# Rows of x1 transposed by VectorE in the down stage's last pass instead of by TensorE in the attention

## The chip, the core and the metric

The kernel runs on one core of a Trainium2 chip. Its time is the device time of one execution in microseconds; the median of three runs counts. The engines are TensorE (PE, with its weight loads as PEld), VectorE (DVE), ScalarE (ACT), GpSimd (POOL) and SyncE (SP). SP, ACT and POOL also issue DMA transfers, each from a queue of its own that issues in order.

## The reference

One decoder layer over 16 sequences of 112 rows with 1024 columns, all in float32 but for the last product:

```
s  = silu(x @ w_gate.T)                     # 1792 rows x 2752
s  = s with the 1376 largest |s| of each row set to 0
x1 = layernorm(x + (s * (x @ w_up.T)) @ w_down.T)
q  = x1 @ Wq ; k, v = ctx @ Wk, ctx @ Wv    # 32 heads of 32, 8 key and value heads, 375 keys
x2 = layernorm(x1 + softmax(q k^T / sqrt(32)) v @ Wo)
out = layernorm(x2 + bf16(x2) @ bf16(dequantized 4-bit weights))
```

`x1` is needed twice: by rows, for the sum behind the attention, and with its columns on the partitions, as an operand of `x1 @ Wq`.

## The kernel before

The 1792 rows are 14 tiles of 128. The stages follow each other: gates with a search for each row's threshold, keys and values, up-projection, down-projection, attention with the last product. Every engine executes its instructions in the order in which the program was written (`as_written`); SP's and ACT's queues therefore issue their transfers in that order too.

**The down stage** (`Down`) takes the tiles in seven pairs j, and computes with sums of blocks in three passes. The last pass (`last_pass`, L652) does for each pair:

- `load_rest(j + 1)` (L646): SP loads two blocks `h` of the next pair from memory (640 KB and 48 KB each, L532 and L533), and DVE adds them (`combine`, L553 and L554). The buffers are those of the pair before, so a load has to wait for that pair's products. The next pair's first product uses the sum.
- the first product p, 11 matmuls of 128x512 (L546); DVE adds it to the second halves of both tiles' rows y0 and y1 (L683, L684); `norm(j, 0)` normalizes y0 on DVE (L72 to L80, with one step on POOL, L75), and POOL stores it to `x1_d` (L672).
- `load_rows(j + 1)` (L659): SP loads the next pair's rows of `x` (L662).
- the second product q; DVE subtracts it from the first half of y1 (L689); `norm(j, 1)`.
- `add_rows(j + 1)` (L665): POOL adds three partial results, `c11`, `v` and `u`, to the next rows (L668, four adds).
- the steps of `beside[j]`. Eight of them unpack the 4-bit weights on DVE (`compute` in `unpack_steps`, L716): a cast, and twice four shifts, one subtraction (L727) and one multiplication (L728). They stand at pairs 1, 1, 2, 3, 4, 4, 5, 6. Their loads are 17 small transfers on ACT's queue each (`load`, L706), at pairs 0, 0, 1, 1, 2, 3, 4, 4. ACT also loads `wq` in four parts.

**x1 transposed** (`Queries`, L735). A group is two sequences, 224 rows. `fetch` (L743) loads one sequence's 112 rows from `x1_d` by ACT's queue into `xr`, of which there is one buffer. `rows` (L748) lets PE transpose them in eight blocks of 112x128 (L757) and ACT copy them from PSUM to `x1T` (L758). `chunk` (L760) multiplies one of eight parts of `wq` with the group's `x1T` (8 matmuls of 224 columns, L765). Group 0 is fetched and turned inside the last pass (`beside[4]` to `beside[6]`), so the transposes stand in PE's order between the products of pair 5 and pair 6 and behind those of pair 6. Three chunks follow, and then the attention.

**The attention** runs 128 units n. Each has four score matmuls (L832), maxima on DVE (L838), exponentials on ACT (L840), a division on POOL (L849) and a 32x32 transposition on DVE (L860); every second unit, 16 transfers (11 on SP, 5 on POOL, L874) put the squares in place for the values' matmuls (L887). The chunks of the next groups, the projection with `wo` (L924), the norms and the last product (L975) are put between the units. At its start SP loads keys (L811), values (L815), `wo` in 16 parts (L999), and then the next keys. The remaining fetches and transposes of x1 stand between the units as well (L1071 to L1078).

Of the kernel before, what the change touches and what calls it, by code (L numbers as in the profile page):

```python
# [10 lines left out]
F32 = mybir.dt.float32  # L11
# [11 lines left out]
P = 128  # L23
B, S, D = 16, 112, 1024
NT = B * S
TT = NT // P
KC = D // P
# [3 lines left out]
Q = 32  # L31
NKQ = -(-SK // Q)
SKP = NKQ * Q
NKP = -(-SK // P)
NH, NKV, HD = 32, 8, 32
REP = NH // NKV
KVD = NKV * HD
GB = 2
GT = GB * S
# [431 lines left out]
class Down:  # L471
# [12 lines left out]

    def __init__(self, nc, tc, negh, wd, hT_d, x, x1_d, ps):
        self.nc, self.tc, self.negh, self.wd, self.hT_d = nc, tc, negh, wd, hT_d
        self.x, self.x1_d, self.ps = x, x1_d, ps
        self.pairs = TT // 2  # L490
        self.parts = {"11": [], "21": []}
        self.asked = [(b, k) for b in ("11", "21") for k in range(HK)]
        self.n_blocks = 0
        self.live = {}
# [154 lines left out]
        self.combine(self.nc.vector, a21, a21, a22, ALU.add)  # L649
        self.live[j] = a21, a22  # L650

    def last_pass(self, beside):  # L652

        nc = self.nc
        with ExitStack() as ctx:
            ld = ctx.enter_context(self.tc.tile_pool(name="d_ld", bufs=4, side="right"))
            small = ctx.enter_context(self.tc.tile_pool(name="d_small", bufs=2, side="right"))

            def load_rows(j):  # L659
                ys = [ld.tile([P, D], F32, tag="y", name=f"y_{j}_{i}") for i in range(2)]  # L660
                for i, y in enumerate(ys):
                    nc.sync.dma_start(y, self.x[ts(2 * j + i, P), :])  # L662
                return ys

            def add_rows(j, ys):  # L665
                for i, h, c in ((0, 0, self.c11), (0, 1, self.v), (1, 1, self.u), (1, 0, self.u)):
                    y = ys[i][:, ts(h, 512)]
                    nc.gpsimd.tensor_tensor(y, y, c[j], ALU.add)  # L668

            def norm(j, i, y):  # L670
                layer_norm(nc, small, y, y, self.negh)
                nc.gpsimd.dma_start(self.x1_d[ts(2 * j + i, P), :], y)  # L672

            rows = {0: load_rows(0)}
            add_rows(0, rows[0])
            for j in range(self.pairs):
# [6 lines left out]
                nc.vector.tensor_add(y0[:, 512:], y0[:, 512:], p)  # L683
                nc.vector.tensor_add(y1[:, 512:], y1[:, 512:], p)  # L684
                norm(j, 0, y0)
                if j + 1 < self.pairs:
                    rows[j + 1] = load_rows(j + 1)
                self.product(q, a22, lambda k: self.chunk("21", k))
                nc.vector.tensor_tensor(y1[:, :512], y1[:, :512], q, ALU.subtract)  # L689
# [45 lines left out]
class Queries:  # L735


    def __init__(self, nc, tc, ctx, ident, x1_d, wq_sb, bank):
        self.nc, self.ident, self.x1_d, self.wq_sb, self.bank = nc, ident, x1_d, wq_sb, bank
        self.pool = ctx.enter_context(tc.tile_pool(name="q_work", bufs=1, side="right"))  # L740
        self.x1T, self.qT, self.xr = {}, {}, {}

    def fetch(self, g, bb):  # L743

        self.xr[g, bb] = self.pool.tile([S, D], F32, tag="xr", name=f"xr_{g}_{bb}")
        self.nc.scalar.dma_start(self.xr[g, bb], self.x1_d[ds((g * GB + bb) * S, S), :])

    def rows(self, g, bb):  # L748
        nc = self.nc
        if bb == 0:  # L750
            self.x1T[g] = self.pool.tile([P, KC, GT], F32, tag="x1T", name=f"x1T_{g}")
            self.qT[g] = self.pool.tile([P, KC, GT], F32, tag="qT", name=f"qT_{g}", bufs=2)
        xr = self.xr.pop((g, bb))
        for k0 in range(0, KC, 4):
            pt = self.bank()[:, : 4 * S].rearrange("p (k s) -> p k s", k=4)
            for k in range(4):
                nc.tensor.transpose(pt[:, k, :], xr[:, ts(k0 + k, P)], self.ident[:S, :S])  # L757
            nc.scalar.copy(self.x1T[g][:, k0 : k0 + 4, ts(bb, S)], pt)  # L758

    def chunk(self, g, mc):  # L760

        nc = self.nc
        pq = self.bank()
        for kc in range(KC):
            nc.tensor.matmul(  # L765
                pq[:, :GT], self.wq_sb[:, kc, ts(mc, P)], self.x1T[g][:, kc, :],
                start=(kc == 0), stop=(kc == KC - 1),
            )
        nc.scalar.activation(self.qT[g][:, mc, :], pq[:, :GT], AF.Copy, scale=SCALE)


def attention_and_ffn(nc, tc, ident, ident_b, negh, x1_d, k_d, v_d, queries, wf_sb, wo, out):
# [16 lines left out]
    with ExitStack() as ctx:  # L789
# [201 lines left out]
        per_group = n_units // (B // GB)  # L991
# [9 lines left out]


        asked, behind, light = deque((0, mc) for mc in range(EARLY, KC)), deque(), {}
        turned, fetched = GB, GB
        sums, tails = {}, {}
        done = soon = 0

# [45 lines left out]
        for n in range(n_units):  # L1053
            b, c, r = units[n]
            if n % 4 == 1 and n // 4 + 1 < 2 * B:
                load_keys(*divmod(n // 4 + 1, 2))
            sums[n] = scores(n)
            if n:
                normalize(n - 1, sums.pop(n - 1))
            if n > 1:  # L1060
                square(n - 2)

            due = asked and n >= asked[0][0] * per_group + asked[0][1] - 2
            if due or (not piece(n) and asked):
                queries.chunk(*asked.popleft())
            if n == 0:
                queries.chunk(*asked.popleft())
            if n > LAG and (n - LAG) % 2:
                attend(n - LAG)

            if not asked and turned < B and n >= (turned // GB - 1) * per_group:  # L1071
                queries.rows(turned // GB, turned % GB)
                turned += 1
                if turned % GB == 0:
                    asked.extend((turned // GB - 1, mc) for mc in range(KC))
            if fetched == turned < B:
                queries.fetch(fetched // GB, fetched % GB)
                fetched += 1  # L1078
            lights(n)
            if done + len(tails) < soon and Tail.live < 3:  # L1080
                tails[done + len(tails)] = Tail(done + len(tails))
# [39 lines left out]
def kernel(  # L1121
# [29 lines left out]
    k_d = dram.tile([B, P, 2, SK], F32, tag="k", name="k_d")  # L1151
    v_d = dram.tile([B, SKP, KVD], F32, tag="v", name="v_d")
    x1_d = dram.tile([NT, D], F32, tag="x1", name="x1_d")

    hT_d = [dram.tile([P, 2 * HK, P], F32, tag=f"h{t}", name=f"hT_d{t}") for t in range(TT)]
    with as_written(nc, tc):
        with ExitStack() as psum:
            ps_g = psum.enter_context(tc.tile_pool(name="ps_g", bufs=6, space=PSUM))
            ps_t = psum.enter_context(tc.tile_pool(name="ps_t", bufs=2, space=PSUM))
            with ExitStack() as left:  # L1160
                down = Down(nc, tc, negh, wd, hT_d, x, x1_d, ps_g)
# [8 lines left out]
                queries = Queries(nc, tc, ctx, ident, x1_d, wq_sb, lambda: down.bank("pq"))  # L1170
                with tc.tile_pool(name="q", bufs=2, side="right") as q_pool:

                    def load_wq(i):
                        nc.scalar.dma_start(wq_sb[:, :, ts(i, D // 4)], wq[:, :, ts(i, D // 4)])

                    loads, computes = unpack_steps(nc, q_pool, wf_sb, qw, qs, qz)
                    beside = [[] for _ in range(TT // 2)]
                    for i, j in enumerate((1, 1, 2, 3, 4, 4, 5, 6)):
                        beside[j].append(computes[i])
                    for i, j in enumerate((0, 0, 1, 1, 2, 3, 4, 4)):  # L1180
                        beside[j].append(loads[i])
                    for i in range(4):
                        beside[i // 2].append(lambda i=i: load_wq(i))
                    beside[4].append(lambda: queries.fetch(0, 0))
                    beside[5] += [lambda: queries.rows(0, 0), lambda: queries.fetch(0, 1)]
                    beside[6].append(lambda: queries.rows(0, 1))
                    down.last_pass(beside)
            for mc in range(EARLY):
                queries.chunk(0, mc)
        attention_and_ffn(nc, tc, ident, ident_b, negh, x1_d, k_d, v_d, queries, wf_sb, wo, out)  # L1190
# [48 lines left out]
```

## Time and profile before

| | |
|---|---|
| median of three runs | 2656.92 us (2655.61 to 2657.28) |
| the profiled execution | 2661.48 us, span 2659.7 us, mean granted clock 0.983 |
| PE, DVE, ACT, POOL busy | 97%, 65%, 52%, 40% of the span |
| last pass of the down stage | from about 1735 us to 1891 us of the span |
| first scores of the attention | 1901.95 us |
| last scores | 2595.7 us |
| transposes of x1 on PE | 128, in 16 blocks of 8, from 1868.2 to 2463.2 us |
| copies of them on ACT | 32, 0.54 us each |

Times in the profile are microseconds from the start of the span, and L numbers are lines of the kernel. A group's row gives the operation, what it writes and reads, how often, and its mean duration. The views of waits say which instruction stood still until which other one had ended; for SP, what its queue waited for before it could issue. Windows give each engine's busy time, the granted clock and the share of the DMA engines in a stretch.

### The profile page before, as it was taken

What the parts mean: (1) busy time and instruction counts of PE and PEld (TensorE: products, weight loads), DVE (VectorE), ACT (ScalarE), POOL (GpSimd) and SP (SyncE); (2) the same over time, 40 slices, a digit from 0 to 9 for tenths busy, and PEclk for the clock granted to TensorE, in tenths of its full rate; (3) what the DMA queues carried; (4) which work ended last, traced back from release to release, by engine and by line L of the source; (5) the groups of instructions that cost most, each with busy time, mean ns of one, the idle gap of its engine ahead of it and who ended that gap; (6) DMA issues with size and microseconds to landing.
All of it is one profiled execution on the core that took longest, in us unless ns stands there. A gap on an engine that the chain in (4) does not pass through costs nothing.

```text
span 2659.7 us, 33179 instructions
## 1 busy us (share of the span) xinstructions
PE 2584.9 (97%) x10266; PEld 1482.7 (56%) x10266; DVE 1730.8 (65%) x3579; ACT 1377.6 (52%) x2413; POOL 1053.8 (40%) x1097
## 2 busy tenths in 40 slices
PE   9999999999999999999999999998899999999997
PEld 4444444577776555555554444443556666667663
DVE  0478778866876788788730343158467777777773
ACT  0487787777767777787610000000255555565553
POOL 0002022213322444344450000023277888788783
PEclk9999999999999999999999999999889999999998
DMA  6221223154443543443346222166567777777763
GB/s 253 94 74 56 77 91 126 51 195 168 181 169 136 162 140 121 143 132 117 95 145 228 86 96 94 59 204 202 133 169 196 196 191 193 192 205 194 188 175 103
DMA packets 216960, 387.70 MB, mean 146 GB/s; under 512 B 32080, under 2 KB 151120, under 8 KB 212688
## 3 DMA queue, kind: packets, MB, share of 16 engines
q1 hardware_dynamic: 165456, 257.19, 32.3%
q0 software_dynamic: 35840, 100.59, 11.6%
q10 hardware_dynamic: 15488, 27.80, 3.5%
q8 instruction: 83, 1.36, 0.2%
q14 instruction: 93, 0.76, 0.1%
HBM read 208.36 MB, written 76.43 MB: 107 GB/s over the span
## 4 chain that ended last, share of the span: by engine, by line
PE 90%; DVE 3%; DMA 3%; ACT 2%; issue 1%; POOL 1%; ACTq 0%; SPq 0%; POOLq 0%; DVEq 0%
PE pg L146 20%; PE pu L234 19%; PE m L546 14%; PE bank L924 7%; PE pk L184 6%; PE pk L176 6%; PE bank L765 6%; PE sc L832 4%; PE po L887 3%; PE bank L975 2%; PE pt L255 1%; ACT probs L840 1%; DVE b L727 1%; DMA xr<-x_d 1%; DVE nmax L838 1%
## 5 line engine op out<-in xcount | busy, mean ns | idle before, releaser
L284 ACT ACTIVATE ja<-a,cand 128x1824 int8<-128x1824 f32 x434 | 788.6, 1817 | 178.4 <-DVE cand L296 174.4
L287 DVE TENSOR_SCALAR_CACHE_REDUCE jv<-a,cand 128x928 uint8<-128x928 f32 x434 | 510.0, 1175 | 56.9 <-ACT a L271 48.8
L234 PE MATMUL pu<-wu_sb,uxT 128*128 128x512 f32 (+1 forms) x1344 | 530.6, 548 | 0.0
L146 PE MATMUL pg<-wg_sb,gxT 128*128 128x456 f32 (+1 forms) x1344 | 519.9, 550 | 5.9 <-DMA wg_sb<-in_wg_dram 5.9
L840 ACT ACTIVATE probs<-sc,nmax 128x375 f32<-128x375 f32 x512 | 287.4, 573 | 237.6 <-DVE nmax L838 218.2
L146 PEld LDWEIGHTS pg<-wg_sb,gxT 128*128 128x128 f32 x1344 | 256.2, 191 | 268.8 <-issue 265.3
L849 POOL TENSOR_TENSOR probs<-probs,sums 128x1500 f32<-128x1500 f32 x128 | 344.2, 2689 | 142.4 <-DVE sums L848 123.2
L234 PEld LDWEIGHTS pu<-wu_sb,uxT 128*128 128x128 f32 x1344 | 249.0, 190 | 230.0 <-issue 188.4
L838 DVE TENSOR_REDUCE nmax<-sc 128x2 f32<-128x750 f32 x256 | 228.6, 932 | 150.3 <-PE sc L832 150.2
L546 PE MATMUL m<-wd,h 128*128 128x512 f32 (+1 forms) x616 | 268.0, 597 | 0.0
L860 DVE STREAM_TRANSPOSE squares<-probs 128x1536 f32<-128x1536 f32 x128 | 224.0, 1750 | 9.7 <-DMA weights<-squares 5.5
L155 POOL DMA_DIRECT2D s_d<-s x84 | 46.0, 548 | 427.4 <-DVE s L154 351.5
L765 PE MATMUL bank<-x1T,wq_sb 128*128 128x224 f32 x976 | 202.6, 361 | 0.0
L546 PEld LDWEIGHTS m<-wd,h 128*128 128x128 f32 (+1 forms) x616 | 117.5, 191 | 149.2 <-issue 145.1
L765 PEld LDWEIGHTS bank<-x1T,wq_sb 128*128 128x128 f32 x976 | 181.3, 191 | 33.2 <-issue 30.2
L924 PE MATMUL bank<-wo_sb,aT 128*128 128x256 f32 x832 | 195.0, 388 | 0.0
L758 ACT COPY x1T<-pq 128x448 f32<-128x448 f32 x4 | 2.0, 535 | 371.6 <-PE pq L757 371.6
L874 POOL DMA_DIRECT2D weights<-squares x320 | 178.6, 564 | 9.0 <-issue 6.6
L924 PEld LDWEIGHTS bank<-wo_sb,aT 128*128 128x128 f32 x832 | 155.4, 192 | 46.5 <-issue 24.9
L184 PE MATMUL pk<-wv_sb,ctx 128*128 128x256 f32 (+1 forms) x768 | 168.4, 379 | 0.0
L176 PE MATMUL pk<-ctx,wk_sb 128*128 128x375 f32 x512 | 164.4, 478 | 0.0
L184 PEld LDWEIGHTS pk<-wv_sb,ctx 128*128 128x128 f32 (+1 forms) x768 | 144.0, 188 | 24.8
(118 smaller groups left out, 2881.8 us busy)
## 6 DMA issues: line engine op xcount, KB each, us to landing
weights<-squares SPq DMA_DIRECT2D x704, 96.0 KB, 3.3
h<-hT_d SPq DMA_DIRECT2D x56, 640.0 KB, 4.5
weights<-squares POOLq DMA_DIRECT2D x320, 96.0 KB, 3.4
ctx<-in_ctxT_dram SPq DMA_DIRECT2D x16, 1500.0 KB, 6.7
a<-s_d SPq DMA_DIRECT2D x14, 1376.0 KB, 7.9
us<-s_d SPq DMA_DIRECT2D x56, 256.0 KB, 2.7
hT_d<-hT POOLq DMA_DIRECT2D x56, 256.0 KB, 3.1
s_d<-s POOLq DMA_DIRECT2D x56, 228.0 KB, 2.2
```

Source lines behind the costliest of these rows:

```text
L146: nc.tensor.matmul(pg[:, :w], xts[t][:, kc, :], wg_sb[:, kc, ds(off, w)], start=(kc == 0), stop=(kc == KC - 1),)
L176: nc.tensor.matmul(pk[:, :SK], wk_sb[:, kc, ts(u, P)], c[:, kc, :], start=(kc == 0), stop=(kc == KC - 1),)
L184: nc.tensor.matmul(pk[:n, :KVD], c[:, kc, ds(at, n)], wv_sb[:, kc, :], start=(kc == 0), stop=(kc == KC - 1),)
L234: nc.tensor.matmul(pu[:, :w], xts[t][:, kc, :], wu_sb[0][:, kc, ds(off, w)], start=(kc == 0), stop=(kc == KC - 1),)
L284: nc.scalar.activation(ja, a[:, NV:], AF.Sign, bias=cand, scale=-1.0, accum_out=st["sgn"])
L287: nc.vector.tensor_scalar(jv, a[:, :NV], cand, -(TOPK - 1 - NA / 2), ALU.is_lt, ALU.add, accum_out=st["nlt"])
L546: self.nc.tensor.matmul(bank, a[:r, k, :], b(k)[:r], start=(k == 0), stop=(k == HK - 1),)
L765: nc.tensor.matmul(pq[:, :GT], self.wq_sb[:, kc, ts(mc, P)], self.x1T[g][:, kc, :], start=(kc == 0), stop=(kc == KC - 1),)
L838: nc.vector.tensor_reduce(nmax[h], sc[h][:, :, :SK], AX.X, ALU.max, negate=True)
L840: nc.scalar.activation(pr[:, i, :SK], sc[i // 2][:, i % 2, :SK], AF.Exp, bias=nmax[i // 2][:, i % 2 : i % 2 + 1], accum_out=sums[:, i : i ...
L849: nc.gpsimd.tensor_tensor(pr, pr, sums.unsqueeze(2).to_broadcast([P, 4, SK]), ALU.mult)
L924: nc.tensor.matmul(pp[:, :256], aT[:, h, r, :], wo_sb[:, h * REP + r, ts(i, 256)], start=(h == 0 and r == 0), stop=(h == 1 and r == REP - 1),)
```

## The change

`x1` is stored a second time, transposed in 32x32 squares, in a new array `x1T_d` of 128 partitions, 56 blocks of 32 rows, 8 parts of columns and 32 rows. In `norm`, after each tile has been normalized, DVE transposes its two halves (128x512 each) square by square, into buffers that are no longer needed (`c11`, `v` and `u` of the pair) and, for the fourth half, into a new one, `x1sq`. Four transfers on SP's queue store each half, one for each 32 partitions: 64 KB each, in runs of 512 bytes.

`Queries.load` takes the place of `fetch` and `rows`: one load of a group (128 partitions of 7 KB, 896 KB) by ACT's queue. The matmul of a chunk reads its 224 columns as seven runs of 32. PE's transposes and ACT's copies are gone. Group 0's load stands at pair 4, later ones in the attention as soon as the chunks of the group before are done; this moves some of the chunks and pieces of projection by a unit.

The steps that unpack weights move from `beside[j]` to `amid[j]`: after y0's norm, ahead of the subtraction of the second product, in the same pairs as before.

```diff
             def norm(j, i, y):
                 layer_norm(nc, small, y, y, self.negh)
-                nc.gpsimd.dma_start(self.x1_d[ts(2 * j + i, P), :], y)
+                t = 2 * j + i
+                nc.gpsimd.dma_start(self.x1_d[ts(t, P), :], y)
+                to = self.x1T_d.rearrange("(m p) b k f -> p m b k f", p=Q)
+                n = KC // 2
+                for h in range(2):
+                    sq = ((self.c11[j], self.v[j]), (self.u[j], None))[i][h]
+                    if sq is None:
+                        sq = ld.tile([P, 512], F32, tag="sq", name=f"x1sq_{t}", bufs=1)
+                    sq = sq.rearrange("p (m k f) -> p m k f", m=SQ, f=Q)
+                    nc.vector.transpose(
+                        sq, y[:, ts(h, 512)].rearrange("p (k m f) -> p m k f", m=SQ, f=Q)
+                    )
+                    for b in range(SQ):
+                        nc.sync.dma_start(to[:, :, t * SQ + b, ts(h, n)], sq[ts(b, Q)])
...
                 norm(j, 0, y0)
+                for step in amid[j]:
+                    step()
                 if j + 1 < self.pairs:
                     rows[j + 1] = load_rows(j + 1)
...
-    def fetch(self, g, bb):
-
-        self.xr[g, bb] = self.pool.tile([S, D], F32, tag="xr", name=f"xr_{g}_{bb}")
-        self.nc.scalar.dma_start(self.xr[g, bb], self.x1_d[ds((g * GB + bb) * S, S), :])
-
-    def rows(self, g, bb):
...
-        for k0 in range(0, KC, 4):
-            pt = self.bank()[:, : 4 * S].rearrange("p (k s) -> p k s", k=4)
-            for k in range(4):
-                nc.tensor.transpose(pt[:, k, :], xr[:, ts(k0 + k, P)], self.ident[:S, :S])
-            nc.scalar.copy(self.x1T[g][:, k0 : k0 + 4, ts(bb, S)], pt)
+    def load(self, g):
+
+        n = GT // Q
+        self.x1T[g] = self.pool.tile([P, n, KC, Q], F32, tag="x1T", name=f"x1T_{g}")
+        self.nc.scalar.dma_start(self.x1T[g], self.x1T_d[:, ts(g, n)])
...
             nc.tensor.matmul(
-                pq[:, :GT], self.wq_sb[:, kc, ts(mc, P)], self.x1T[g][:, kc, :],
+                pq[:, :GT].rearrange("p (b f) -> p b f", f=Q), self.wq_sb[:, kc, ts(mc, P)],
+                self.x1T[g][:, :, kc, :],
...
-            if not asked and turned < B and n >= (turned // GB - 1) * per_group:
-                queries.rows(turned // GB, turned % GB)
-                turned += 1
-                if turned % GB == 0:
-                    asked.extend((turned // GB - 1, mc) for mc in range(KC))
-            if fetched == turned < B:
-                queries.fetch(fetched // GB, fetched % GB)
-                fetched += 1
+            if not asked and group < B // GB:
+                if group not in queries.x1T:
+                    queries.load(group)
+                elif n >= (group - 1) * per_group:
+                    asked.extend((group, mc) for mc in range(KC))
+                    group += 1
...
-                    beside = [[] for _ in range(TT // 2)]
+                    amid, beside = ([[] for _ in range(TT // 2)] for _ in range(2))
                     for i, j in enumerate((1, 1, 2, 3, 4, 4, 5, 6)):
-                        beside[j].append(computes[i])
+                        amid[j].append(computes[i])
...
-                    beside[4].append(lambda: queries.fetch(0, 0))
-                    beside[5] += [lambda: queries.rows(0, 0), lambda: queries.fetch(0, 1)]
-                    beside[6].append(lambda: queries.rows(0, 1))
-                    down.last_pass(beside)
+                    beside[4].append(lambda: queries.load(0))
+                    down.last_pass(amid, beside)
```

More of the change, by code (lines that the diff above doesn't have):

```diff
@@ L34 @@
 NKP = -(-SK // P)
+SQ = P // Q
 NH, NKV, HD = 32, 8, 32
@@ L471, with __init__ @@
 class Down:
-    def __init__(self, nc, tc, negh, wd, hT_d, x, x1_d, ps):
+    def __init__(self, nc, tc, negh, wd, hT_d, x, x1_d, x1T_d, ps):
         self.nc, self.tc, self.negh, self.wd, self.hT_d = nc, tc, negh, wd, hT_d
-        self.x, self.x1_d, self.ps = x, x1_d, ps
+        self.x, self.x1_d, self.x1T_d, self.ps = x, x1_d, x1T_d, ps
         self.pairs = TT // 2
@@ L650, in load_rest, with last_pass @@
         self.live[j] = a21, a22
-    def last_pass(self, beside):
+    def last_pass(self, amid, beside):
         nc = self.nc
@@ L735, with __init__ @@
 class Queries:
-    def __init__(self, nc, tc, ctx, ident, x1_d, wq_sb, bank):
-        self.nc, self.ident, self.x1_d, self.wq_sb, self.bank = nc, ident, x1_d, wq_sb, bank
+    def __init__(self, nc, tc, ctx, x1T_d, wq_sb, bank):
+        self.nc, self.x1T_d, self.wq_sb, self.bank = nc, x1T_d, wq_sb, bank
         self.pool = ctx.enter_context(tc.tile_pool(name="q_work", bufs=1, side="right"))
-        self.x1T, self.qT, self.xr = {}, {}, {}
-    def fetch(self, g, bb):
-        self.xr[g, bb] = self.pool.tile([S, D], F32, tag="xr", name=f"xr_{g}_{bb}")
-        self.nc.scalar.dma_start(self.xr[g, bb], self.x1_d[ds((g * GB + bb) * S, S), :])
-    def rows(self, g, bb):
[L749 to L753, printed above, removed]
-        for k0 in range(0, KC, 4):
-            pt = self.bank()[:, : 4 * S].rearrange("p (k s) -> p k s", k=4)
-            for k in range(4):
-                nc.tensor.transpose(pt[:, k, :], xr[:, ts(k0 + k, P)], self.ident[:S, :S])
-            nc.scalar.copy(self.x1T[g][:, k0 : k0 + 4, ts(bb, S)], pt)
+        self.x1T, self.qT = {}, {}
+    def load(self, g):
+        n = GT // Q
+        self.x1T[g] = self.pool.tile([P, n, KC, Q], F32, tag="x1T", name=f"x1T_{g}")
+        self.nc.scalar.dma_start(self.x1T[g], self.x1T_d[:, ts(g, n)])
     def chunk(self, g, mc):
         nc = self.nc
+        if g not in self.qT:
+            self.qT[g] = self.pool.tile([P, KC, GT], F32, tag="qT", name=f"qT_{g}", bufs=2)
         pq = self.bank()
@@ L1003, in attention_and_ffn @@
         asked, behind, light = deque((0, mc) for mc in range(EARLY, KC)), deque(), {}
-        turned, fetched = GB, GB
+        group = 1
         sums, tails = {}, {}
@@ L1153 @@
     x1_d = dram.tile([NT, D], F32, tag="x1", name="x1_d")
+    x1T_d = dram.tile([P, NT // Q, KC, Q], F32, tag="x1T", name="x1T_d")
     hT_d = [dram.tile([P, 2 * HK, P], F32, tag=f"h{t}", name=f"hT_d{t}") for t in range(TT)]
@@ L1160 @@
             with ExitStack() as left:
-                down = Down(nc, tc, negh, wd, hT_d, x, x1_d, ps_g)
+                down = Down(nc, tc, negh, wd, hT_d, x, x1_d, x1T_d, ps_g)
                 gates_keys_up(
@@ L1169 @@
                 wf_sb = a_w.tile([P, 8, D], BF16, tag="wf", name="wf_sb")
-                queries = Queries(nc, tc, ctx, ident, x1_d, wq_sb, lambda: down.bank("pq"))
+                queries = Queries(nc, tc, ctx, x1T_d, wq_sb, lambda: down.bank("pq"))
                 with tc.tile_pool(name="q", bufs=2, side="right") as q_pool:
```

## The prediction

> **What bounds the kernel now.** I read the page's engine shares and its chain first, to see whether TensorE (PE) sets the time.
>
> ```profile
> PE 2584.9 (97%) x10266; PEld 1482.7 (56%) x10266; DVE 1730.8 (65%) x3579; ACT 1377.6 (52%) x2413; POOL 1053.8 (40%) x1097
> PE 90%; DVE 3%; DMA 3%; ACT 2%; issue 1%; POOL 1%; ACTq 0%; SPq 0%; POOLq 0%; DVEq 0%
> ```
>
> PE bounds nearly everything. The change touches the last pass of the down stage and the attention, so I next asked for busy time by stretch:
>
> ```profile
> 1812.00:1831.00 19.00, 19.00 (x45) 8.21 (x45) 17.23 (x29) 0.00 (x0) 7.23 (x8) 1.00 0.78 260
> 1850.00:1868.00 18.00, 0.00 (x0) 0.00 (x0) 16.26 (x28) 0.00 (x0) 7.21 (x8) 0.61 0.31 101
> 1902.00:1930.00 28.00, 21.19 (x124) 18.00 (x128) 10.77 (x14) 13.08 (x40) 10.79 (x8) 0.92 0.74 171
> 2350.00:2550.00 200.00, 199.69 (x1433) 142.16 (x1432) 152.31 (x197) 117.91 (x371) 165.74 (x152) 1.00 0.77 198
> ```
>
> (Columns: length; PE, PEld, DVE, ACT, POOL busy; clock; DMA share; GB/s.) In the last pass PE is full, and VectorE (DVE) is busy 17.2 of 19 us, nearly a second bound. PE then stands still for 18 us, and again for 7 us where the attention starts; later it is full. The waits of 1763 to 1903 us name the first hole:
>
> ```profile
> PE pq L757 <- DMA xr<-x_d: 18.7, 1, 18.7
> PEld m L546 <- DVE h L553: 2.4, 3, 0.9
> ```
>
> The rows to be transposed arrive late. The products hardly wait for the combined blocks `h`. DVE's timeline over one pair:
>
> ```profile
> 1809.76 1.48 DVE L553 TENSOR_TENSOR h<-h,h 128x1280 f32<-128x1280 f32 x1
> 1811.36 0.68 DVE L683 TENSOR_TENSOR y<-y,m 128x512 f32<-128x512 f32 x1
> 1815.72 0.68 DVE L689 TENSOR_TENSOR y<-y,m 128x512 f32<-128x512 f32 x1
> 1819.57 0.22 DVE L719 CAST zf<-zi 128x128 f32<-128x128 int32 x1
> 1820.37 5.69 DVE L727 TENSOR_TENSOR b<-b,zf 128x512 f32<-128x512 int32 x1
> 1828.82 1.49 DVE L553 TENSOR_TENSOR h<-h,h 128x1280 f32<-128x1280 f32 x1
> ```
>
> The lap is 19.06 us: combine 1.60, adds and first norm 4.36, subtraction and second norm 3.85, unpacking 9.25. PE needs 18.9 (22 products of 128x512 at 0.859, from 1754.4 to 1773.3). The laps just fit. Last I asked what SP's queue waits for, because the change puts stores there:
>
> ```profile
> SPq L811 <- PE m L546: 28.2, 1, 28.2
> SPq L532 <- DMA zi<-in_qz_dram: 21.4, 3, 15.6
> SPq L533 <- DMA sc<-in_qs_dram: 13.6, 3, 5.6
> SPq L811 <- DMA xr<-x_d: 9.9, 1, 9.9
> ```
>
> Loads of `h` wait for small loads of another queue that they don't use: in the built order each transfer from SP or ACT waits for the one eight before it. `h` waits so, with q, y and further zi and sc, 51.3 us over seven pairs, about 7 each. Today that is hidden.
>
> **PE transposes and ScalarE copies go.** Sixteen blocks of eight transposes leave PE: 14 in the attention at 0.93 us (row at 1921.66) are 13.0 us of a full PE, with 10.7 us of waits for `xr` (5.6 and 5.1). Two leave the last pass, with the 18.7 us hole and about 2.5 us in which PE then ran at half clock (clock 0.50 from 1868 to 1874; the products took 21.4 us instead of 18.9). 32 copies of 0.54 us leave ACT, which isn't the bound: nothing.
>
> **VectorE gains 56 instructions, four per pair.** The attention's L860 takes 1750 ns for 1536 columns, so 512 columns take 0.58 us; 0.69 is the upper end (a 512-column add). I take 0.58: 2.33 us per pair.
>
> On the Trainium skill: the page "VectorE: DVE Perf Modes", section "Rules for kernel authors", advises TensorE for a 128x128 transpose where PSUM will do. Its section "The three transpose paths" gives 311 ns on VectorE against 390 on TensorE for a bf16 block. By those figures eight blocks in each of 14 tiles would gain an estimated 9 us. This trace has 116 ns a block on PE (0.93/8) and 146 on DVE (1.17/8), so by the rows the move loses 3.4 us of engine time. The measurement decides; neither figure is used below.
>
> **Unpacking moves ahead of the second product's subtraction.** Each of eight blocks has 14 DVE instructions and no DMA. Beside POOL's adds its L727 takes 5.69 us, alone 0.69; the undisturbed block from 1786.42 to 1790.67 took 4.25. POOL's adds now fall after the second norm, beside transposes and a wait, so I take 4.25 (up to 9.25 if they still meet). The move delays the second norm by 4.25, or 8.5 in pairs 1 and 4, which unpack twice.
>
> **112 stores join SP's queue, and they carry the cost.** Per pair SP now issues: stores of y0 (8), loads of the next y (2), stores of y1 (8), and only then the `h` loads (4) for the pair after next. Before, the `h` loads waited for PE alone and came a lap early. Now they stand behind stores that wait for the second norm, the combine waits for `h`, and all DVE work of the next lap stands behind the combine. A store of 64 KB isn't in the trace. Issue lies between 0.37 (the `h` load) and 0.65 (weights on SP, eleven in 7.11 us); I take 0.65, also 32 partitions per transfer. Landing is 2.2 to 3.3 us.
>
> The new lap, combine to combine: 1.60 + 4.36 + two transposes 1.17 + unpacking 4.25 + 3.85 + one transpose 0.58 = 15.8 us to the first y1 store; then 8 x 0.65 = 5.2, four issues 1.5, landing 4.4 (median here): 26.9. To this come the eight-back waits. At least 0, at most some 10, since 16 transfers of about 3 us share the rotation with today's 7; I take 5, below today's 7, since some of those waits overlap the stores: **32 us a lap**. With two unpackings, 4.25 more for DVE and 2.2 for the second set of 17 loads: **38.5**.
>
> The second norm of pair 0 ends at 1758.4. One transpose, 11.1 of return and 5 of waits put pair 2's combine at 1775 (before: 1761.6). Laps of 38.5, 32, 32 and 38.5 bring pair 6's to 1916, and its first product to 1917.7. Before it began at 1869.7: **+48.0**. The two products then take 21.4 as before, after idle time as before.
>
> **The keys stand behind the last stores.** Before, kT was issued at 1891.18, as the last product ended. Now subtraction and norm 3.85, a transpose 0.58 and eight stores 5.2 come first: 9.6 later. The three query chunks (9.35 us) cover the first keys but for 1.2 us. The second keys follow the 16 wo loads (24.2 us), and PE already waits 6.8 for them, so all **+9.6** shows.
>
> **One x1T load of 896 KB per group replaces two of 448.** Landing lies between 4.8 (`xr`) and 7.9 (1376 KB rows). Each holds one of the eight places for longer, and keys and weights wait behind. The attention gains at most 23.7 and loses at worst 10. I keep the 13.0 and give 8 back: **-5.0**. Query products now read seven runs of 32 columns; L887, which also reads such runs, takes 391 ns against 388 contiguous, so nothing (1.7 us at most). Group 0's load is issued two products before its use and is covered.
>
> **Sum:** 48.0 + 9.6 - 5.0 = +52.6 us. The profiled run took 2661.48 (span 2659.7, 1.8 around it), 4.6 above the median 2656.92. A profile of the new kernel should show some 2714; the median becomes 2709.
>
> **Rivals.**
> - *The return trip is hidden: faster.* Should `h` go out early enough, PE's 18.9 remain, the hole goes, and the last product ends at 1868.4 instead of 1891.1: -22.7 + 9.6 - 23.7 = -36.8, 2620 us. It decides where the four laps fall below 22.1 us on average ((141 - 52.6)/4). For it: today `h` goes out early. Against: 15.8 + 5.2 + 1.5 + 4.4 is already above.
> - *A bare return, without eight-back waits.* Laps of 26.9 and 31.2 from 1770 put the last combine at 1886.2, its product at 1887.9: +18.2 + 9.6 - 5.0 = +22.8, 2680 us. For it: landings can be 2.2 us. Against: the waits of SP shown above.
> - *Waits of 10 a lap.* Laps of 37 and 43.5 from 1780 put the last product at 1942.7: +73.0 + 9.6, with the attention between -5 and +10: 2735 to 2750 us. For it: stores wait for zi and sc loads, and these for stores.
>
> **How the numbers follow.** The round trip with waits of 3 to 8 us: 0.55. Bare: 0.17. Long: 0.16. Hidden: 0.09. Cancelled to within 0.2%: 0.02. Another slower way: 0.01. About 0.2%, 5 us, is what a measurement of this kernel can tell from no change. Slower 0.89, same 0.02, faster 0.09. The range 2664 to 2744 leaves out the hidden case and half of the long one.
>
> **What would show it.** Right: PE idle 10 to 20 us before each of the products of pairs 2 to 6, released by L554's `h`; DVE waiting for `h<-hT_d`; `h` issued after the stores of x1sq; L745 near 0.69 us; kT issued some 10 us after the last product. Wrong: `h` issued during the first product of the lap before, laps near 19 us, or an attention that is longer than before by more than 10 us. The prediction fails if stores issue much faster than 0.65, or the eight-back waits fall beside DVE's work instead of after it.

## The result, and the profile after

The changed kernel takes 2698.1 us (median of four runs, 2697.1 to 2707.7), the kernel before in the same session 2657.1 (2655.6 to 2659.7). The ratio is 1.0161, with a 95% interval of 1.0137 to 1.0186: 41 us slower. The profiled execution of the changed kernel took 2707.71 us (span 2705.9), 9.6 above its median; the sums below are made from it and, as in the prediction, against the profiled execution of before (span 2659.7): +46.2 us.

First the shares of the engines and the chain, from the page of the changed kernel:

```profile
PE 2575.8 (95%) x10124; PEld 1470.4 (54%) x10138; DVE 1724.6 (64%) x3607; ACT 1359.0 (50%) x2381; POOL 1052.6 (39%) x1097
...
PE 84%; DMA 5%; DVE 4%; issue 2%; ACT 2%; SPq 1%; POOL 1%; ACTq 0%; POOLq 0%; DVEq 0%
```

PE's busy time fell by only 9 us, and its share of the chain from 90% to 84%. The time went into waits. Those from 1763 to 1950 us:

```profile
DVE h L554 <- DMA h<-hT_d: 71.3, 5, 17.9
...
PE m L547 <- DVE h L554: 52.2, 5, 19.8
...
PE sc L842 <- DMA kT<-k_d: 9.1, 1, 9.1
```

The one hole of 18.7 us before pair 6 (waiting for `xr`) has become five holes, 52.2 us together: 2.2, 19.8, 7.8, 7.4 and 15.0 before the first products of pairs 2 to 6. In each, PE waits for the combination of `h`, and the combination waits for its load. SP's timeline shows why, for the lap in which pair 4's `h` is fetched:

```profile
1820.02 2.44 SPq L688 DMA_DIRECT2D x1T_d<-c  x4
1822.55 1.85 SPq L688 DMA_DIRECT2D x1T_d<-v  x4
1825.82 1.45 SPq L663 DMA_DIRECT2D y<-in_x_dram  x2
1829.48 3.98 SPq L688 DMA_DIRECT2D x1T_d<-u  x4
1833.56 1.86 SPq L688 DMA_DIRECT2D x1T_d<-x1sq  x4
1835.51 0.39 SPq L533 DMA_DIRECT2D h<-hT_d  x1
...
1836.91 0.43 SPq L534 DMA_DIRECT2D h<-hT_d  x1
```

(Columns: start, duration of the group, queue and line, what is moved.) Stores of y0 (`c`, `v`), rows of the next pair, stores of y1 (`u`, `x1sq`), and `h` last of all. DVE's timeline of the same lap:

```profile
1813.18 1.49 DVE L554 TENSOR_TENSOR h<-h,h 128x1280 f32<-128x1280 f32 x1 [17.91 <-DMA h<-hT_d]
...
1819.28 0.71 DVE L684 STREAM_TRANSPOSE c<-y 128x512 f32<-128x512 f32 x1
...
1821.27 0.69 DVE L745 TENSOR_TENSOR b<-b,zf 128x512 f32<-128x512 int32 x1
...
1828.69 0.71 DVE L684 STREAM_TRANSPOSE u<-y 128x512 f32<-128x512 f32 x1
1829.33 0.67 DVE L684 STREAM_TRANSPOSE x1sq<-y 128x512 f32<-128x512 f32 x1
1841.88 1.49 DVE L554 TENSOR_TENSOR h<-h,h 128x1280 f32<-128x1280 f32 x1 [11.88 <-DMA h<-hT_d]
```

The lap is 28.7 us: 16.2 us of DVE's work up to the first transpose of y1, 6 of stores, 1.8 of issues for `h`, 4.5 until the last part lands. DVE is at its work for 16.8 us, short waits for the norm's step on POOL included, and then stands still for 11.9. The unpacking's L745 takes 0.69 us here, no longer 5.69.

The end of the stage, SP's timeline:

```profile
1945.66 0.40 SPq L821 DMA_DIRECT2D kT<-k_d  x1
1946.10 0.98 SPq L825 DMA_DIRECT2D v<-v_d  x2
1947.13 16.43 SPq L1009 DMA_DIRECT2D wo_sb<-in_wo_dram  x16
...
1976.34 0.35 SPq L821 DMA_DIRECT2D kT<-k_d  x1
```

The keys are issued 15.5 us after the last product's end (1930.2). Before, that was at once.

The table cuts every run at the same three places of its profiled execution: the times between the combinations of pairs 2 to 6, the end of the last product, the first score matmul that uses the second keys, and the end of the span. All in us. The ratios further down are to the kernel before as it was run beside each version (medians 2656.6 to 2658.2).

| run | median | laps | last product ends | to the second keys' scores | from there to the end |
|---|---|---|---|---|---|
| before | 2657.1 | 29.1, 19.1, 19.1, 23.3 | 1891.1 | 38.3 | 730.3 |
| changed | 2698.1 | 39.0, 28.7, 29.3, 35.9 | 1930.2 | 48.6 | 727.1 |
| move of the unpacking alone | 2644.0 | 20.6, 17.0, 22.4, 18.8 | 1876.2 | 39.4 | 729.2 |
| unpacking back | 2689.8 | 32.2, 32.4, 30.4, 31.8 | 1923.5 | 44.5 | 724.1 |
| stores on POOL | 2669.0 | 27.0, 23.8, 22.4, 26.7 | 1885.1 | 59.1 | 719.5 |
| `h` early | 2675.0 | 26.0, 29.7, 26.9, 26.0 | 1902.1 | 48.5 | 723.5 |
| combination late | 2674.3 | 29.1, 26.1, 23.9, 31.1 | 1911.0 | 44.3 | 720.1 |
| `h` early, combination late | 2667.0 | 23.8, 26.2, 23.4, 26.6 | 1896.7 | 46.4 | 718.7 |
| the same, rows first too | 2654.9 | 23.8, 25.7, 23.6, 23.8 | 1890.5 | 42.3 | 719.5 |
| one store per half | 2741.8 | 36.9, 35.2, 34.7, 37.7 | 1944.9 | 61.6 | 733.3 |
| early, late, one store per half | 2710.8 | 24.8, 32.8, 32.3, 27.6 | 1911.9 | 61.9 | 736.1 |
| POOL's stores behind its adds | 2662.0 | 23.3, 21.2, 22.4, 25.4 | 1881.0 | 56.6 | 722.5 |
| last pair's stores on POOL | 2706.8 | 35.2, 29.4, 28.7, 36.5 | 1926.1 | 54.7 | 728.1 |
| reordered | 2668.2 | 25.7, 28.3, 24.4, 26.5 | 1897.4 | 46.2 | 729.0 |

### The profile page after: what moved, and what is told of

It is laid out like the page before. It is cut to its first block, busy times and chain, and to the rows that moved or that the text cites. A ratio compares the mean times of both kernels' runs of the same rounds, so it can differ in the third digit from the quotient of the medians.

```text
span 2705.9 us, 33011 instructions
## 1 busy us (share of the span) xinstructions
PE 2575.8 (95%) x10124; PEld 1470.4 (54%) x10138; DVE 1724.6 (64%) x3607; ACT 1359.0 (50%) x2381; POOL 1052.6 (39%) x1097
## 4 chain that ended last, share of the span: by engine, by line
PE 84%; DMA 5%; DVE 4%; issue 2%; ACT 2%; SPq 1%; POOL 1%; ACTq 0%; POOLq 0%; DVEq 0%
PE pu L235 19%; PE pg L147 19%; PE m L547 13%; PE bank L934 7%; PE pk L185 6%; PE pk L177 6%; PE bank L774 4%; PE sc L842 3%; PE po L897 3%; PE bank L985 2%; DMA h<-hT_d 1%; ACT probs L850 1%; PE pt L256 1%; DVE nmax L848 1%; SPq L884 1%
## 5 line engine op out<-in xcount | busy, mean ns | idle before, releaser
L547 PE MATMUL m<-wd,h 128*128 128x512 f32 (+1 forms) x616 | 275.0, 609 | 52.2 <-DVE h L554 52.2
L842 PE MATMUL sc<-kT,qT 32*128 32x375 f32 x1024 | 140.6, 545 | 26.4 <-DMA kT<-k_d 16.8
```

Of the source, the lines that this page charges most:

```text
L547: self.nc.tensor.matmul(bank, a[:r, k, :], b(k)[:r], start=(k == 0), stop=(k == HK - 1),)
```

## The experiments

The theory was the prediction's: `h` stands in SP's queue behind stores that wait for the second norm, so the lap becomes a round trip. The rivals were that DVE's added work sets the lap, and that the waits of each transfer for the one eight before it do.

**The two halves of the change, each alone.** First the move without transposes and stores:

```diff
 (kernel before)
                 norm(j, 0, y0)
+                for step in amid[j]:
+                    step()
...
-                        beside[j].append(computes[i])
+                        amid[j].append(computes[i])
```

> The kernel before with the unpacking moved between the two products, and nothing else. Theory: the move costs only through the stores that wait for the second norm; without them h goes out early, DVE has 1.6 + 4.4 + 4.25 + 3.85 = 14 us of work in a lap of 18.9, and L727 takes 0.69 instead of 5.69 us. Within 4 us of the kernel before, 2653 to 2661 us. Rival (the move by itself delays the second norm, and with it the next rows and products): laps grow by up to 4 us, 2665 to 2680 us.

Measured: 2644.0 us, ratio 0.9945 (0.9930 to 0.9960). Both expectations missed a gain of 13 us. It is in PE's hole before pair 6, which shrank from 18.68 to 4.20 us, as PE's timelines of before and of the move alone show:

```profile
1868.20 1.73 PE L757 MATMUL pq<-ident,xr 112*128 112x112 f32 x8 [18.68 <-DMA xr<-x_d]
```

```profile
1853.48 1.73 PE L759 MATMUL pq<-ident,xr 112*128 112x112 f32 x8 [4.20 <-DMA xr<-x_d]
```

ACT's queue shows why; before:

```profile
1846.57 0.35 ACTq L710 DMA_DIRECT2D q<-in_qw_dram  x1
...
1855.10 0.38 ACTq L710 DMA_DIRECT2D q<-in_qw_dram  x1
...
1863.57 0.72 ACTq L746 DMA_DIRECT2D xr<-x_d  x1
```

and with the move:

```profile
1831.61 0.36 ACTq L712 DMA_DIRECT2D q<-in_qw_dram  x1
...
1840.73 0.38 ACTq L712 DMA_DIRECT2D q<-in_qw_dram  x1
...
1849.70 0.38 ACTq L748 DMA_DIRECT2D xr<-x_d  x1
```

The fetch of `xr` stands in ACT's queue behind two sets of unpacking loads, and these wait for buffers that earlier unpacking frees: the first load shown goes out at 1846.57 and 1831.61, and the last shift that read its buffer had ended on DVE at 1846.53 and 1831.57. Unpacking earlier frees them earlier, the fetch goes out 13.9 us sooner, and pair 6's first product starts 14.7 us sooner.

Then the transposes and stores without the move (`amid[j].append` back to `beside[j].append`):

> The changed kernel with the unpacking back behind the second norm; transposes and stores stay. Theory (round trip by way of the second norm): a lap loses 4.25 us, two of them 8.5, and the unpacking (9.25 beside POOL's adds) falls into DVE's wait for h of 12 to 18 us, which two of them in one lap overrun by 3 to 5 us. Pair 6's first product comes 20 to 30 us earlier than 1908.6, the keys 4 us earlier: about 2668 to 2678 us. Rival (DVE's work in all sets the lap): the unpacking takes 5 us longer beside the adds, so 2700 to 2720 us.

Measured: 2689.8 us, 1.0113 (1.0096 to 1.0130), a gain of 8.3 us on the changed kernel where 20 to 30 were expected. The laps with two unpackings fell by 6.8 and 4.1 us, those with one grew by 3.7 and 1.1. SP's queue names what took the gain back, in the changed kernel and here (1735 to 1945 us):

```profile
SPq L688 <- DMA y<-in_x_dram: 5.6, 4, 2.3
```

```profile
SPq L688 <- DMA y<-in_x_dram: 23.9, 11, 3.4
```

The stores of y1 come sooner and now wait for the loads of the rows, which they don't use: the waits for the transfer eight before. So the move is worth -13 us without the stores and +8 with them; transposes and stores cost 33 us without the move and 54 with it.

**SP's order, and DVE's.** The stores on another queue:

```diff
-                        nc.sync.dma_start(to[:, :, t * SQ + b, ts(h, n)], sq[ts(b, Q)])
+                        nc.gpsimd.dma_start(to[:, :, t * SQ + b, ts(h, n)], sq[ts(b, Q)])
```

> The changed kernel, with its 112 stores of x1T issued by POOL instead of SP. Theory (the loads of h stand in SP's queue behind stores that wait for the second norm): h goes out as soon as its buffer is free, DVE's waits of 12 to 18 us for it go, and the laps fall from 28.7 to 39 us to what POOL allows: about 4.4 us for eight stores at 0.55 and 5 us of adds behind the last transpose, some 24 us, 28 with two unpackings. The last lap's keys are issued as DVE's last norm ends at the latest. About 2660 to 2675 us. Rival (DVE's own added work sets the lap): laps stay within 2 us of 28.7, about 2690 to 2700 us. Rival (the wait of each transfer for the one eight before it, rather than the order): POOL's transfers are outside that rotation, so this run goes as in the theory and does not tell the two apart; the next one does.

Measured: 2669.0 us, 1.0039 (1.0024 to 1.0054), and laps of 22 to 27 us, as the theory said. DVE did the same work, so its work doesn't set laps of 29 to 39. Whether the order or the waits for the transfer eight before did, this run can't tell, since stores on POOL have part in neither. What ended DVE's waits now (1735 to 1945 us):

```profile
DVE y L699 <- POOL y L669: 32.0, 6, 6.6
```

POOL issues a store in 0.55 us, and its adds stand behind eight of them.

The loads of `h` ahead of the stores, all on SP (the first such load, ahead of the loop, and what makes `load_rest` use the blocks are not shown):

```diff
...
                 self.product(q, a22, lambda k: self.chunk("21", k))
+                if j + 2 < self.pairs:
+                    self.load_blocks(j + 2)
```

> The changed kernel, with the four loads of h for pair j+2 issued right after pair j's second product, ahead of the stores of y1, on the same queue; the combination stays where it was. Theory (order in SP's queue): the return trip goes. DVE's work in a lap is 16.6 us, 20.8 with two unpackings, PE's products 18.9: laps of 19 to 22 us, no wait of DVE for h above 3 us, last product ending near 1872 us of the span instead of 1930; the keys still wait behind the last stores. About 2645 to 2655 us. Rival (the wait for the transfer eight before it): the loads stand behind the eight stores of y0 and two loads of x and wait for those; laps stay above 25 us, about 2680 to 2695 us. Rival (DVE's work sets the lap): laps unchanged, 2698 us.

Measured: 2675.0 us, 1.0058 (1.0043 to 1.0073). 23 us were won where 43 to 53 were expected. The rival's laps came (26.0 to 29.7, above 25), its time of 2680 us or more did not. The theory had overlooked that `h` still stands behind y0's stores, and that DVE's order closes the ring: combination, adds, first norm, stores of y0, rows, `h`, combination. SP's timeline of one such lap shows both the order and the waits for the transfer eight before; four issues of 0.33 us take 5.1:

```profile
1777.29 2.49 SPq L693 DMA_DIRECT2D x1T_d<-c  x4
1779.87 1.84 SPq L693 DMA_DIRECT2D x1T_d<-v  x4
1783.18 1.29 SPq L668 DMA_DIRECT2D y<-in_x_dram  x2
1787.01 0.33 SPq L533 DMA_DIRECT2D h<-hT_d  x1
1788.80 0.34 SPq L534 DMA_DIRECT2D h<-hT_d  x1
1790.84 0.32 SPq L533 DMA_DIRECT2D h<-hT_d  x1
1791.75 0.33 SPq L534 DMA_DIRECT2D h<-hT_d  x1
```

In these programs the transfers of SP and ACT share eight semaphores (marks that a transfer sets when it has landed), and each transfer waits for the mark that it will use. The trace shows what used the marks of these four last: a load of the rows and three unpacking loads. They landed at 1786.95, 1788.79, 1790.76 and 1791.73, each less than 0.1 us ahead of the issue that it held up.

So the combination was moved on DVE (out of `load_rest` into a function `add_rest`, which is not shown), with SP's order left as in the changed kernel:

```diff
                 norm(j, 0, y0)
+                if j + 1 < self.pairs:
+                    self.add_rest(j + 1)
                 for step in amid[j]:
```

> The changed kernel with SP's order left alone; only the combination of h for pair j+1 moves on DVE from ahead of y0's adds to behind y0's norm and transposes of lap j. Theory, after the last runs (the ring needs both orders: SP's, in which h stands behind stores, and DVE's, in which adds and first norm stand behind the combination): the 5.7 us of adds, norm and transposes now run while h lands, the ring becomes stores 5.5, issue 2, landing 4.5, combination 1.6, unpacking 4.2, subtraction, norm and transpose 4.5, together 22.3 and some waits: laps of 23 to 24, 27 to 28 with two unpackings. About 2665 to 2676 us. Rival (SP's order alone sets the lap): still 28.7 and 39, 2698 us.

Measured: 2674.3 us, 1.0071 (1.0055 to 1.0088): in the expected range, though three of the four laps are 1 to 4 us longer than forecast. The ring needs both orders; breaking either wins some 23 us. Both together:

> The changed kernel with both: the loads of h for pair j+2 ahead of y1's stores, and the combination behind y0's norm and transposes. Theory: no ring is left through SP's stores. PE's 18.9 us set the lap, with DVE at 16.6 (20.8 with two unpackings): last product ends at 1868 to 1875 us, keys issued some 10 us later, about 2632 to 2645 us, faster than the kernel before. Rival (the wait for the transfer eight before it sets the lap by itself): as with the early loads alone, laps of 24 us and more, 2660 to 2675 us. Rival (DVE's work): laps of 21 us and more, about 2650 us.

Measured: 2667.0 us, 1.0036 (1.0022 to 1.0049): the rival's numbers. The waits on `h` are nearly gone, but the rows `y` also stand behind y0's stores, and POOL's adds and DVE wait for them (1763 to 1890 us):

```profile
POOL y L673 <- DMA y<-in_x_dram: 20.2, 6, 6.7
```

```profile
DVE y L702 <- POOL y L673: 25.1, 5, 8.8
```

With the rows first as well (`load_rows(j + 1)` moved to the head of the lap):

> Early loads of h and late combination, and now the loads of the next rows too ahead of y0's stores; all stores stay on SP. Theory (order): the last ring was y0's stores, loads of the rows, POOL's adds, y0's adds; with the rows first no load that DVE needs stands behind stores of its own lap. Laps of 19 to 21 us, last product ending at 1868 to 1880, first scores some 17 us later because of the keys behind the stores: 2640 to 2652 us. Rival (the waits for the transfer eight before are a cost of their own, since each load still waits for a store or a small load of ACT's queue): laps of 23 us and more, 2658 us or more.

Measured: 2654.9 us, 0.9984 (0.9973 to 0.9994), the same as before within what can be told. With the order mended, 43 us of the changed kernel's time are won back. Yet the laps are 23.6 to 25.7, not 19 to 21. The rival had said so, but with a time of 2658 us or more. SP's queue still waits for loads that it doesn't use (1763 to 1890 us):

```profile
SPq L692 <- DMA zi<-in_qz_dram: 11.0, 6, 3.1
SPq L692 <- DMA wq_sb<-in_wq_dram: 9.2, 2, 5.6
SPq L692 <- DMA q<-in_qw_dram: 8.0, 2, 4.7
```

DVE's waits in the same stretch show how much of that reaches the laps:

```profile
DVE y L704 <- POOL y L673: 16.2, 6, 4.2
...
DVE h L554 <- DMA sc<-in_qs_dram: 6.0, 1, 6.0
DVE h L554 <- DMA h<-hT_d: 3.9, 1, 3.9
```

The 6.0 and the 3.9 us fall into the two laps with one unpacking, 25.7 and 23.6, which without them would be 19.6 and 19.7. In the two laps with two unpackings, both 23.8, DVE waits for no load at all: it is busy for 19.1 and 19.2 us, and waits 2.6 for POOL's adds and 1.4 for norm steps. So the waits for the transfer eight before explain the single laps; the double ones are DVE's own work and POOL's adds, which the expectation left out. To move a transfer also changes which one stands eight places before it, so these runs don't part order and waits to the last microsecond. The late combination, which leaves SP's order as it was and won 24 us, comes closest.

**The number of stores.** One store of 256 KB per half, and four loads per group:

```diff
...
-                    for b in range(SQ):
-                        nc.sync.dma_start(to[:, :, t * SQ + b, ts(h, n)], sq[ts(b, Q)])
+                    to = self.x1T_d[:, ts(t, SQ), h].rearrange("p b c -> b p c")
+                    nc.sync.dma_start(to, sq)
...
```

> The changed kernel with one store of 256 KB for each transposed half instead of four of 64 KB, and four loads of x1T per group instead of one. Theory (the path from the second norm over SP's stores to h sets the lap): eight stores of y1 took 5 to 6 us to issue, two take about 1.2, so each lap loses some 4 us, also some of the waits for the transfer eight before; laps 28.7 to about 24.5, 39 to 35; the keys come 3 us earlier. About 2668 to 2680 us. Rival (what counts is that a store is there at all, or the bytes): within 5 us of 2698.

> The early loads of h, the late combination and one store per half together. Theory: laps are PE's already, so only the keys gain, 2 to 3 us, and the attention pays or gains up to 3 us for four loads of x1T per group: 2628 to 2642 us. Rival (the waits of eight still set the laps with early loads): a gain of 10 us and more over the run with early loads and late combination.

Measured: 2741.8 us, 1.0322 (1.0304 to 1.0339), and 2710.8 us, 1.0206 (1.0191 to 1.0222): 44 us slower each than with four stores (34 and 48 in the profiled executions), where both theories had a gain. With a quarter of the issues it got worse, in all three parts of the table. SP's waits, changed kernel and one store per half (1735 to 1945 us):

```profile
SPq L688 <- DMA sc<-in_qs_dram: 19.9, 5, 7.1
```

```profile
SPq L685 <- DMA sc<-in_qs_dram: 46.1, 6, 13.1
SPq L685 <- DMA zi<-in_qz_dram: 11.8, 4, 6.0
...
SPq L534 <- DMA zi<-in_qz_dram: 10.7, 4, 4.1
```

With 16 stores a pair, most of SP's transfers have another SP transfer eight places before them, by these marks in the trace 92 of 143 from 1750 to 1945 us. With four, that place mostly holds a transfer of ACT (46 of 60 from 1750 to 1960 us), 41 times a small unpacking load, which itself waits for others. That this explains the whole 44 us is argued from these waits, not shown: only 15 us of the loss lies before the last product's end, in each of the two kernels, and the loads of a group in four parts and the pattern of the larger store changed with it.

**The keys behind the last stores.** Only the last pair's stores on POOL:

```diff
-                        nc.sync.dma_start(to[:, :, t * SQ + b, ts(h, n)], sq[ts(b, Q)])
+                        queue = nc.gpsimd if j + 1 == self.pairs else nc.sync
+                        queue.dma_start(to[:, :, t * SQ + b, ts(h, n)], sq[ts(b, Q)])
```

> The changed kernel, with only the last pair's sixteen stores of x1T on POOL. Theory: the laps stay as they were; the keys no longer stand behind the last stores and go out at the last product's end instead of 15.5 us later. The first scores then wait for DVE's last subtraction, 6.4 us behind PE, instead of for keys: about 9 us earlier, and the second keys with them: 2687 to 2692 us. Rival (the keys' delay is covered by query products and by the loads of wo, so that it costs little): within 4 us of 2698.

Measured: 2706.8 us, 1.0173 (1.0153 to 1.0193): no gain, where 2687 to 2692 us were expected. The median is 8.7 us above the changed kernel's, the profiled execution 2.8. The keys went out as the last product ended, and the first scores started 9.7 us after it instead of 18.4, as expected. Then PE waited 14.2 us for the exponentials, because DVE had to wait to clear `probs`:

```profile
1937.76 0.67 DVE L684 STREAM_TRANSPOSE x1sq<-y 128x512 f32<-128x512 f32 x1
1953.55 0.15 DVE L817 MEMSET probs<- 128x108 f32 x1 [15.12 <-DMA wo_sb<-in_wo_dram]
```

In the run with all stores on POOL behind its adds the same instruction waited 10.6 us, there for the last store of `x1sq`; in the changed kernel, with SP's stores, 5.7. Here the row names a `wo` load, because that landed last, but the trace shows that POOL's last store held `probs`. The store was issued only at 1946.84, after waits of its own, and landed at 1952.99; DVE passed the wait for it at 1953.02, and the waits behind it followed 0.1 us apart. The late keys are thus one of two ends that come close together.

**Towards a faster version.** POOL's stores with those of y1 behind the adds:

> The changed kernel with its stores of x1T on POOL, as in the run with POOL's stores, but those of y1 behind POOL's adds to the next rows. Theory: with the stores on POOL the loads no longer stand behind them, and what was left was DVE's wait of 6 us a lap for adds that stood behind eight stores; with the adds first, DVE's lap is 16.6 us and about 1 of waits, below PE's 18.9. Laps of 19 to 20, last product ending at 1868 to 1875 us, keys issued then, first scores about 1880: 2628 to 2640 us, faster than the kernel before and than the move of the unpacking alone (2644). Rival (DVE's added work or POOL's time binds): laps above 21 us, 2645 us or more.

Measured: 2662.0 us, 1.0011 (1.0003 to 1.0020). Laps of 21 to 25, the rival's side, because the adds now run beside the combination, which takes four times as long:

```profile
1806.37 5.95 DVE L554 TENSOR_TENSOR h<-h,h 128x1280 f32<-128x1280 f32 x1
```

The last version put the combination elsewhere, the adds ahead of y1's store, y1's stores behind the next first norm, and the last pair's stores on SP:

> The changed kernel with the orders that the runs so far point to: stores of x1T on POOL for pairs 0 to 5 and on SP for the last pair; POOL's adds to the next rows ahead of these stores and of the store of y1; the stores of y1 put behind the next pair's first norm; the combination behind that norm, away from POOL's adds. Theory: no load stands behind stores, no add behind eight stores, and the combination takes 1.5 us instead of the 5.95 that it took beside the adds. Laps of 19 to 20 us, 22 to 23 with two unpackings, last product ending at 1870 to 1878; from there to the second keys' scores 42 us as in the run with the loads first, and 722 from there to the end: about 2632 to 2645 us, level with the move of the unpacking alone (2644) or some us below. Rival (POOL's own stores and DVE's added work hold the lap above 21 us): 2648 us or more.

Measured: 2668.2 us, 1.0038 (1.0023 to 1.0054), the rival's side. Now the adds met the second norm's scaling, 0.81 us alone:

```profile
1811.30 5.42 DVE L81 TENSOR_SCALAR y<-y,ln_mv,ln_rstd 128x1024 f32<-128x1024 f32 x1 [7.54 <-POOL ln_rstd L76]
```

and its 7.54 us of waiting are for a norm step on POOL behind sixteen stores. The fastest version found is the move of the unpacking alone, 2644.0 us, which beats both kernels.

## Why the prediction was right, and where not

The forecast was 2709 us, slower; 2698.1 was measured. Its sum was +52.6 on the profiled execution, and +46.2 came: 39.1 up to the last product's end (predicted 48.0), 10.3 from there to the second keys' scores (9.6), -3.2 after that (-5.0).

- *The return trip*: right. `h` is issued behind y1's stores, PE stands still before every pair from 2 to 6, always for L554. Only two of the five holes (19.8 and 15.0 us) lie within the 10 to 20 that the prediction named as its sign; the others are 2.2 to 7.8. Taking the stores off SP, the loads ahead of them, or the combination out of the ring's way each took 23 to 29 us off. What the prediction saw only in part is that the ring runs through DVE's order too, and that the rows are in a second ring.
- *The lap's terms*: pair 2's combination came at 1774.2 (1775 predicted). The bare lap of 26.9 was right within a microsecond. The mis-sized term is the 5 us of eight-back waits: single laps took 28.7 and 29.3 instead of 32, so 1.8 and 2.4. They sit in the four stores of `u`, which took 3.98 and 4.08 us instead of 1.9. The loads of `h` hardly waited there: of the transfers eight before them, two were stores of `u` and two small unpacking loads, and these had landed. So the run lies below the waits of 3 to 8 us a lap that the prediction's likeliest case asked for. The double laps took 39.0 and 35.9 for 38.5; in the first, `h` took 9.5 us to land beside two loads of `wq` instead of 4.4.
- *Stores of 0.65 us*: 0.46 to 0.6 without waits. *Transposes of 0.58 us*: 0.71 and 0.67, 1.23 for two from start to end. By duration that is 172 ns a block against PE's 116, so here VectorE is the slower. The Trainium skill, page "VectorE: DVE Perf Modes", section "The three transpose paths", has it the other way round for a bf16 block (311 ns against 390 on TensorE); the rows decide for these float32 blocks. The prediction's "56 instructions" are 28, four in each of seven pairs; its 2.33 us per pair has the right number.
- *Keys*: issued 15.5 us after the last product instead of 9.6, since DVE ran 6 us behind PE: its adds for pair 6 waited 2.1 us for POOL, until 1925.9, and the unpacking stood before the last subtraction. PE waited 9.1 us for the first keys, not 1.2. The sum of the step, 10.3 for 9.6, is right by luck, as two errors cancel: the 16 `wo` loads took 16.4 us instead of 24.2.
- *Attention*: -3.2 in this execution. Over the ten profiles that have the four stores a half and the one load of x1T, the stretch from the second keys to the end took 718.7 to 729.0 us, 723.2 on average, against 730.3 and 729.2 with PE's transposes. So -5.0 was a fair value, and the full 13.0 never came. Whether the larger load of x1T is the reason, as the prediction had it, no run shows.
- *Unpacking*: L745 at 0.69 as predicted. But the sum treated the move as a cost alone. Without the stores it is a gain of 13 us, because it lets `xr` be fetched earlier. The prediction credited the hole's end to the transposes that leave; either half of the change ends it or nearly so (4.20 us were left with the move alone).
- *Rivals*: hidden return (2620) and waits of 10 a lap (2735 to 2750) did not occur. The bare return gave laps of 26.9 and 31.2: the single laps lie nearer to it than to the forecast, the double ones don't.

## What to carry to other kernels

Before stores are added to a queue, list what stands behind them there, and follow that on to the engine that waits for it: a load that waits for nothing becomes a round trip once it stands behind a store of the lap's last result. Such a ring can be broken in more than one place, here in SP's order or in DVE's, and the next ring is close behind. Measure the halves of a change apart: here one half was worth 13 us, and the other turned it into a loss.

## What the runs showed that was not expected

- A transfer on SP waits for unrelated ones of ACT's queue, and fewer transfers can go with more of these waits: 4 instead of 16 stores a pair cost 44 us, twice, though that the waits are the whole cause is not shown.
- POOL's adds stall DVE for their whole length: beside four adds of 1.25 us, L727 took 5.69 us instead of 0.69, the combination 5.95 instead of 1.49, a scaling of one tensor 5.42 instead of 0.81. The Trainium skill, page "SBUF — State Buffer", section "Who interferes with whom", says that GpSimd and VectorE share a port pair as an exclusive lock, that a VectorE instruction with two inputs in SBUF contends for it with a GpSimd instruction that reads SBUF, and that one in a two-port mode contends too. The rows of L727 and of the combination, with two inputs each, agree; in which mode the scaling ran, no run here shows. A transpose that the first add overlapped by 0.4 us in the changed kernel kept its 0.67.
- Memory that is reused counts as an order too: `probs` could only be cleared once the last transfers from the memory beneath it had landed, which with the last pair's stores on POOL cost more than the earlier keys had won.
